# A graph layer on one core: 320 products an edge, selectors that carry all four parts of e, sums turned by VectorE, and a wait of POOL at every other batch

## The chip, the core and the metric

The kernel runs on one core of one Trainium2 chip. The metric is the device time of one execution in microseconds. Three runs of the kernel before took 4756.0, 4765.0 and 4784.8 us; the median is 4765.0 us. Five engines matter: TensorE (PE in the profile; PEld is its weight load), VectorE (DVE), ScalarE (ACT), GpSimd (POOL) and SyncE (SP), which only issues transfers. Matmul results land in PSUM, everything else stands in SBUF.

## The reference

There are 12500 nodes with 160 features and 400000 edges, sorted by destination. A layer norm and a relu come first; the rest, cut to what matters, is:

```python
x0 = h[:, :64];  x1 = h[:, 64:].reshape(n, 32, 3)
y0 = x0 @ W_l1_0 * a / 8
y1 = einsum('nuc,uv->nvc', x1, W_l1_1) * a / sqrt(32)
w = silu(e16 @ fc_W1 / 4) @ fc_W2 / 8            # 192 weights an edge: w_a, w_b (64), w_c, w_d (32)
ys0, ys1 = y0[src], y1[src]                       # the row of the source node
e0, e1 = e4[:, :1], e4[:, 1:]                     # four parts of e
mid_a = w_a * ys0 * e0
mid_d = w_d * einsum('euc,ec->eu', ys1, e1) / sqrt(3)
mid_b = (w_b * ys0)[:, :, None] * e1[:, None, :]
mid_c = (w_c * e0)[:, :, None] * ys1
z0 = zeros((n, 96)).at[dst].add(concat([mid_a, mid_d], 1)) / sqrt(10)
z1 = zeros((n, 96, 3)).at[dst].add(concat([mid_b, mid_c], 1)) / sqrt(10)
out = x + skip(h) + [z0 @ W_l2_0, z1 @ W_l2_1] * a * constants
```

Every edge thus has a weight row (192 numbers), a gathered row of y (160 numbers) and four numbers e. Their products are summed over the edges of a destination.

## The kernel before, in words

The edges lie in 3125 tiles of 128. Four tiles make a batch; there are 782 batches. A first part (the node steps, up to about 115 us) norms the nodes and writes y to memory (`y_d`); in the background the weights are loaded by SP. Then comes the loop over batches, whose order on every engine is written out by hand (a manual schedule): an engine takes its instructions in the order of the program.

In iteration b of that loop stand, in this order:

- `weigh(b + 2)`: PE makes the 192 weights of the batch after next in PSUM (tile `pw`, two buffers; line 606). Then `scale` lets ACT multiply the first 96 weights of each tile by e0 (line 524, four instructions) and copy the other numbers of e and the place in the window into `pw` (line 525).
- for the first three batches of a group the steps `turn`, `linear` and `add` of the group before it: `turn` transposes the sums by PE against an identity (line 656) and ACT copies them (`za`, line 658); `linear` multiplies them by the last weights `wo` (line 665); `add` moves them to their nodes (line 677). `accumulate` lets VectorE add them to `acc` (line 688).
- some work on nodes beside it (the skip path; rows of 16 batches that are computed instead of gathered).
- `select(b + 1)` and `products(b + 1)` on VectorE. `select` makes, for each edge, a 32-wide one-hot row of its place in a window of 32 nodes (line 618) and three copies of it multiplied by e1 (line 620): tile `sel`, 4 x 32 columns. `products` makes 256 products an edge (tile `pr`): lines 530 and 532 for the dot product of ys1 and e1, line 533 for w_b ys0, line 534 for w_a ys0, line 535 for w_c ys1, line 537 for mid_d.
- `sums(b)`: for each tile one matmul of `sel` (stationary, 128 columns) with `pr` (moving, 256 columns) into a window's PSUM tile `pz` (two buffers; line 640). Quadrant 3 of `pz` then holds the sums under the plain one-hot and quadrants 0 to 2 those times e1, of which only parts are used. A window takes 24 tiles at the start of the sorted edges and 3 at their end. When one ends, ACT copies the four useful pieces to `zs` (lines 646 and 648). Four windows are a group.
- `gather(b + 4)`: POOL issues four indirect DMAs (line 573), one a tile, each for 128 rows of y. The first of them waits for the last matmul of `sums(b)` (lines 576 to 579). Each also waits until VectorE has left its buffer of `yg` (six buffers).
- at every fourth batch `hidden_pair`: PE and ACT make the hidden layer for four batches (lines 586 and 591).

fp32 matmuls stand twice in the profile, so 3125 calls at line 640 are 6250 records. A last part of the kernel (from line 892) handles edges outside their window in a loop that runs zero times or once.

Of the kernel before, what the change touches and what calls it, by code (L numbers as in the profile page):

```python
# [10 lines left out]
F32 = mybir.dt.float32  # L11
I32 = mybir.dt.int32
AF = mybir.ActivationFunctionType
# [12 lines left out]
PC = 256  # L26
ZC = 384
# [23 lines left out]
def kernel(  # L51
# [85 lines left out]
    wo = const.tile([P, 3, D], F32, name="wo")  # L137
# [11 lines left out]
    wor = ip.tile([P, 3, D], F32, name="wor")  # L149
# [115 lines left out]
    def edge_weight_loads():  # L265
# [14 lines left out]
        load(wor[0:M0 + M1, 0, 0:M0], w_l2_0)  # L280
        for rows, k, c in ((slice(96, P), 0, 0), (slice(0, 32), 1, 1), (slice(32, 64), 1, 2)):
            load(wor[rows, k, o1(c)], w_l2_1[M0:, :])
        for rows, k, c in ((slice(64, P), 1, 0), (slice(0, 64), 2, 1), (slice(64, P), 2, 2)):
            load(wor[rows, k, o1(c)], w_l2_1[0:M0, :])
# [5 lines left out]
    def edge_weights():  # L290
# [3 lines left out]
        nc.vector.tensor_scalar(wo[M0:M0 + M1, 0, 0:M0], wo[M0:M0 + M1, 0, 0:M0], 1.0 / math.sqrt(3.0), None, ALU.mult)  # L294
# [226 lines left out]
    def scale(pw, ev, n):  # L521

        for k in range(n):
            nc.scalar.activation(pw[:, k, 0:96], pw[:, k, 0:96], AF.Copy, scale=ev[:, k, 0:1])  # L524
        nc.scalar.activation(pw[:, :n, NW:NW + 4], ev[:, :n, 1:5], AF.Copy)  # L525

    def multiply(pr, tmp, wt, yg, n):

        y1 = yg[:, :n, M0:].rearrange("p t (c u) -> p t c u", c=3)
        nc.vector.tensor_tensor(tmp[:, :n, 0:3, :], y1, wt[:, :n, NW:NW + 3].unsqueeze(3).to_broadcast([P, n, 3, M1]),  # L530
                                ALU.mult)
        nc.vector.tensor_reduce(tmp[:, :n, 3, :], tmp[:, :n, 0:3, :].rearrange("p t c u -> p t u c"), AX.X, ALU.add)  # L532
        nc.vector.tensor_mul(pr[:, :n, 192:PC], wt[:, :n, 96:160], yg[:, :n, 0:M0])  # L533
        nc.vector.tensor_mul(pr[:, :n, 0:M0], wt[:, :n, 0:M0], yg[:, :n, 0:M0])  # L534
        nc.vector.tensor_mul(pr[:, :n, 96:192].rearrange("p t (c u) -> p t c u", c=3),  # L535
                             wt[:, :n, M0:96].unsqueeze(2).to_broadcast([P, n, 3, M1]), y1)
        nc.vector.tensor_mul(pr[:, :n, M0:96], wt[:, :n, 160:NW], tmp[:, :n, 3, :])  # L537

    with (
        tc.tile_pool(name="selp", bufs=4) as selp,  # L540
        tc.tile_pool(name="prod", bufs=3) as prod,
        tc.tile_pool(name="tmp", bufs=1) as tmpp,
# [8 lines left out]
        hids, rows, wts, sels, z_ps, z_sb, zT, o_sb, prs, sums_ps, summed = ({} for _ in range(11))  # L551
# [16 lines left out]
        def gather(b):  # L568
# [3 lines left out]
            for k, t in enumerate(tiles_of(b)):  # L572
# [3 lines left out]
                if k == 0 and b - AHEAD in summed:  # L576
# [37 lines left out]
        def select(b):  # L614

            n, wt = slots_of(b), wts[b]
            sel = sels[b] = selp.tile([P, GT, 4, WN], F32, name="sel")[:, :n, :, :]
            nc.vector.tensor_tensor(sel[:, :, 3, :], iota[:, 0:WN].unsqueeze(1).to_broadcast([P, n, WN]),  # L618
                                    wt[:, :n, NW + 3:NW + 4].to_broadcast([P, n, WN]), ALU.is_equal)
            nc.vector.tensor_tensor(sel[:, :, 0:3, :], sel[:, :, 3:4, :].to_broadcast([P, n, 3, WN]),  # L620
                                    wt[:, :n, NW:NW + 3].unsqueeze(3).to_broadcast([P, n, 3, WN]), ALU.mult)

        def products(b):
            wt, yg = wts.pop(b), rows.pop(b)
            pr = prod.tile([P, GT, PC], F32, name="pr")
            tmp = tmpp.tile([P, GT, 4, M1], F32, name="tmp")
            multiply(pr, tmp, wt, yg, slots_of(b))
            prs[b] = pr

        def sums(b):  # L630
# [3 lines left out]
            for k, t in enumerate(tiles_of(b)):  # L634
# [397 lines left out]
```

## Time and profile before

| | |
|---|---|
| median of three runs | 4765.0 us |
| the profiled execution | 4775.0 us, of which the span of its instructions is 4773.1 us |
| batches, tiles, gathers by POOL, windows | 782, 3125, 3061, 598 |
| share of the span that PE, DVE, ACT, POOL are busy | 78%, 62%, 46%, 62% |
| mean busy share of the 16 DMA engines in the loop | about 25% |

The page of the profile gives, in its second part, the share that every engine is busy in 40 equal slices. Nearly all slices look alike:

```profile
PE   7777778787777777777777777778777887788877
DVE  5666666666666666656566656656566666666655
ACT  5333334344444443444444444444444455555555
POOL 5666666666656666666666666656665666665655
```

So no engine is busy throughout, and there is no stage that is much different from the others; ACT has more to do towards the end, where windows are short. A row of the fifth part names a line of the kernel, an engine, the operation, the tiles written and read, shapes and count, then busy time in us and the mean of one in ns, and after the second bar the time that the engine was idle right before such instructions and what ended it ("issue" is an end that the profile doesn't explain by another instruction, "remote" a semaphore whose writer it doesn't know). The timeline lists instructions in order of time with start, length, and in brackets the idle time before them.

### The profile page before, as it was taken

The numbers are of one execution on the slowest core, as the hardware profiler recorded it, in microseconds if no ns is written. First come the engines' busy times: TensorE is split into PE (matmuls) and PEld (weight loads), VectorE is DVE, ScalarE is ACT, GpSimd is POOL, SyncE is SP. The second block draws the span as 40 slices with busy tenths as digits, with TensorE's granted clock in tenths as the row PEclk, the third lists the DMA queues.
The fourth block names the chain that finished last, engine by engine and source line by source line (L and its number), as shares of the span: only waits on it lengthen the run. The fifth ranks groups of instructions, "written<-read, shape, count | busy, mean of one in ns | idle before, by whom it ended". The sixth has DMA issues, their size and how long they took to land.

```text
span 4773.1 us, 53679 instructions
## 1 busy us (share of the span) xinstructions
PE 3720.7 (78%) x13928; PEld 2551.0 (53%) x13928; DVE 2953.5 (62%) x8027; ACT 2205.2 (46%) x7512; POOL 2962.3 (62%) x3145
## 2 busy tenths in 40 slices
PE   7777778787777777777777777778777887788877
PEld 6455555455555554555555555555555555555555
DVE  5666666666666666656566656656566666666655
ACT  5333334344444443444444444444444455555555
POOL 5666666666656666666666666656665666665655
PEclk8888888888988888888888888888888888988988
DMA  7222222222222222222222222222222222222224
GB/s 192 67 60 64 63 62 65 60 65 66 61 62 65 66 70 66 66 63 69 65 69 63 66 62 64 67 62 64 62 66 65 64 66 63 68 66 66 64 58 115
DMA packets 262414, 328.99 MB, mean 69 GB/s; under 512 B 82776, under 2 KB 212104, under 8 KB 262104
## 3 DMA queue, kind: packets, MB, share of 16 engines
q0 software_dynamic: 150128, 256.23, 21.8%
q1 hardware_dynamic: 111478, 69.00, 5.2%
q8 instruction: 113, 1.85, 0.2%
q14 instruction: 197, 1.61, 0.1%
q10 hardware_dynamic: 498, 0.30, 0.0%
HBM read 307.66 MB, written 17.61 MB: 68 GB/s over the span
## 4 chain that ended last, share of the span: by engine, by line
PE 56%; another core or an unknown queue 15%; ACT 12%; issue 8%; DVE 7%; POOL 0%; DMA 0%; DVEq 0%; SPq 0%; ACTq 0%
PE pz L640 23%; PE pw L606 17%; ACT pw L524 6%; PE px L586 6%; PE px L665 3%; ACT zs L648 2%; PE px L656 2%; PE px L677 2%; DVE tmp L532 1%; DVE tmp L530 1%; ACT zs L646 1%; DVE pr L535 1%; DVE pr L534 1%; ACT pw L525 1%
## 5 line engine op out<-in xcount | busy, mean ns | idle before, releaser
L573 POOL DMA_INDIRECT yg<-y_d,src_q x3061 | 2896.2, 946 | 1748.8 <-issue 787.3
L640 PE MATMUL pz<-pr,sel 128*128 128x256 f32 x6250 | 1682.1, 417 | 38.1 <-ACT zs L648 36.1
L606 PE MATMUL pw<-w,hT 128*128 128x384 f32 x3126 | 1314.2, 547 | 304.3 <-DVE pr L537 111.7
L524 ACT ACTIVATE pw<-pw,ev 128x96 f32<-128x96 f32 x3125 | 984.9, 315 | 1199.1 <-remote 303.9
L640 PEld LDWEIGHTS pz<-pr,sel 128*128 128x128 f32 x6250 | 1289.4, 214 | 279.0 <-ACT zs L648 46.4
L606 PEld LDWEIGHTS pw<-w,hT 128*128 128x128 f32 x3126 | 619.2, 208 | 822.5 <-issue 377.2
L618 DVE TENSOR_TENSOR sel<-iota,pw 128x128 f32<-128x128 f32 x782 | 221.5, 283 | 1255.8 <-ACT pw L525 680.1
L646 ACT ACTIVATE zs<-pz 32x192 f32<-32x192 f32 x598 | 193.4, 323 | 801.0 <-remote 345.2
L532 DVE TENSOR_REDUCE tmp<-tmp 128x128 f32<-128x384 f32 x782 | 463.6, 593 | 31.1 <-remote 3.6
L586 PE MATMUL px<-xe,w 32*128 32x512 f32 x782 | 334.2, 750 | 161.0 <-ACT za L658 102.8
L620 DVE TENSOR_TENSOR sel<-sel,pw 128x384 f32<-128x384 f32 x782 | 432.7, 553 | 39.8 <-remote 8.0
L530 DVE TENSOR_TENSOR tmp<-yg,pw 128x384 f32<-128x384 f32 x766 | 419.6, 548 | 55.4 <-DMA yg<-y_d,src_q 48.8
L535 DVE TENSOR_TENSOR pr<-pw,yg 128x384 f32<-128x384 f32 x766 | 419.2, 547 | 0.0
L648 ACT ACTIVATE zs<-pz 32x64 f32<-32x64 f32 x1794 | 383.1, 214 | 24.4
L656 PE MATMUL px<-ident,zs 128*128 128x128 f32 (+1 forms) x450 | 129.3, 362 | 301.3 <-ACT zs L646 259.2
L533 DVE TENSOR_TENSOR pr<-pw,yg 128x256 f32<-128x256 f32 x766 | 317.0, 414 | 0.0
L534 DVE TENSOR_TENSOR pr<-pw,yg 128x256 f32<-128x256 f32 x766 | 316.9, 414 | 0.0
L591 ACT ACTIVATE hT<-px 128x512 f32<-128x512 f32 x391 | 216.1, 594 | 212.2 <-PE px L586 86.7
L656 PEld LDWEIGHTS px<-ident,zs 128*128 128x128 f32 (+1 forms) x450 | 69.7, 159 | 411.9 <-ACT zs L646 307.7
L586 PEld LDWEIGHTS px<-xe,w 32*128 32x128 f32 x782 | 90.2, 218 | 282.3 <-ACT za L658 123.4
L665 PEld LDWEIGHTS px<-wo,za 128*128 128x128 f32 x900 | 163.6, 222 | 108.0 <-ACT hT L591 36.2
L537 DVE TENSOR_TENSOR pr<-pw,tmp 128x128 f32<-128x128 f32 x782 | 219.2, 280 | 0.0
(139 smaller groups left out, 2210.2 us busy)
## 6 DMA issues: line engine op xcount, KB each, us to landing
yg<-y_d,src_q POOLq DMA_INDIRECT x3061
xe<-in_e SPq DMA_DIRECT2D x784, 32.0 KB
xs<-in_x SPq DMA_DIRECT2D x48, 160.0 KB
acc<-in_x SPq DMA_DIRECT2D x11, 640.0 KB
y_d<-ys SPq DMA_DIRECT2D x11, 640.0 KB
out<-acc SPq DMA_DIRECT2D x11, 640.0 KB
raw<-in_e SPq DMA_DIRECT2D x32, 192.0 KB
src_q<-in_src SPq DMA_DIRECT2D x32, 48.0 KB
```

The costliest lines, as they stand in the source:

```text
L524: nc.scalar.activation(pw[:, k, 0:96], pw[:, k, 0:96], AF.Copy, scale=ev[:, k, 0:1])
L530: nc.vector.tensor_tensor(tmp[:, :n, 0:3, :], y1, wt[:, :n, NW:NW + 3].unsqueeze(3).to_broadcast([P, n, 3, M1]), ALU.mult)
L532: nc.vector.tensor_reduce(tmp[:, :n, 3, :], tmp[:, :n, 0:3, :].rearrange("p t c u -> p t u c"), AX.X, ALU.add)
L533: nc.vector.tensor_mul(pr[:, :n, 192:PC], wt[:, :n, 96:160], yg[:, :n, 0:M0])
L534: nc.vector.tensor_mul(pr[:, :n, 0:M0], wt[:, :n, 0:M0], yg[:, :n, 0:M0])
L535: nc.vector.tensor_mul(pr[:, :n, 96:192].rearrange("p t (c u) -> p t c u", c=3), wt[:, :n, M0:96].unsqueeze(2).to_broadcast([P, n, 3, M1]) ...
L573: fetch = nc.gpsimd.indirect_dma_start(out=yg[:, slot(t), :], out_offset=None, in_=y_d, in_offset=bass.IndirectOffsetOnAxis(ap=ev4[t // BL ...
L586: nc.tensor.matmul(ph, w1[r, :], xe[r, :], start=True, stop=True)
L606: nc.tensor.matmul(pw[:, 2 * k:2 * k + m, 0:NW], hT[:, o:o + P], w2[:, :m, :], start=True, stop=True)
L620: nc.vector.tensor_tensor(sel[:, :, 0:3, :], sel[:, :, 3:4, :].to_broadcast([P, n, 3, WN]), wt[:, :n, NW:NW + 3].unsqueeze(3).to_broadcast ...
L640: mm = nc.tensor.matmul(pz[:, 0:PC], sel[:, slot(t), :, :], pr[:, slot(t), :], start=o == 0, stop=last)
L648: nc.scalar.activation(zs[:, 192 + M0 * c:192 + M0 * (c + 1)], pz[WN * c:WN * (c + 1), 192:PC], AF.Copy)
```

## The change

Products are 320 an edge in place of 256, and they are no longer multiplied by any part of e. The products are w_a ys0 (64), w_c ys1 (96), w_b ys0 (64) and w_d ys1 (96). The selector `sel` now has four 32-wide parts: the one-hot row times e0 and times each part of e1. One matmul of 320 columns gives all sums for all four parts; the useful squares are picked when they are turned. The multiplication by e0 on ACT is gone, and so is the dot product on VectorE: both now happen in the sum and in `wo`, which has five slices of 128 rows in place of three.

When a window ends, VectorE transposes its PSUM tile in squares of 32 straight into `za` (two instructions, 128 x 160 and 32 x 160). ACT's copies to `zs`, PE's transposes and ACT's copy of these are gone. `turn` as a step is gone; `linear` and `add` stand at the second and third batch of a group as before, and `linear` has five matmuls.

POOL waits for sums only where b is even. Three more small loads of weights are issued by SP in the node steps.

```diff
-PC = 256
-ZC = 384
+PC = 320
+ZC = 448
+ZK = 5
...
     def scale(pw, ev, n):
-        for k in range(n):
-            nc.scalar.activation(pw[:, k, 0:96], pw[:, k, 0:96], AF.Copy, scale=ev[:, k, 0:1])
-        nc.scalar.activation(pw[:, :n, NW:NW + 4], ev[:, :n, 1:5], AF.Copy)
+        nc.scalar.activation(pw[:, :n, NW:NW + 5], ev[:, :n, :], AF.Copy)
...
     def multiply(pr, wt, yg, n):
         y1 = yg[:, :n, M0:].rearrange("p t (c u) -> p t c u", c=3)
-        nc.vector.tensor_tensor(tmp[:, :n, 0:3, :], y1, wt[:, :n, NW:NW + 3].unsqueeze(3).to_broadcast([P, n, 3, M1]),
-                                ALU.mult)
-        nc.vector.tensor_reduce(tmp[:, :n, 3, :], tmp[:, :n, 0:3, :].rearrange("p t c u -> p t u c"), AX.X, ALU.add)
-        nc.vector.tensor_mul(pr[:, :n, 192:PC], wt[:, :n, 96:160], yg[:, :n, 0:M0])
-        nc.vector.tensor_mul(pr[:, :n, 0:M0], wt[:, :n, 0:M0], yg[:, :n, 0:M0])
-        nc.vector.tensor_mul(pr[:, :n, 96:192].rearrange("p t (c u) -> p t c u", c=3),
-                             wt[:, :n, M0:96].unsqueeze(2).to_broadcast([P, n, 3, M1]), y1)
-        nc.vector.tensor_mul(pr[:, :n, M0:96], wt[:, :n, 160:NW], tmp[:, :n, 3, :])
+        nc.vector.tensor_mul(pr[:, :n, :].rearrange("p t (x u) -> p t x u", x=2)[:, :, :, 0:M0],
+                             wt[:, :n, 0:NW].rearrange("p t (x u) -> p t x u", x=2)[:, :, :, 0:M0],
+                             yg[:, :n, 0:M0].unsqueeze(2).to_broadcast([P, n, 2, M0]))
+        for x in range(2):
+            nc.vector.tensor_mul(pr[:, :n, D * x + M0:D * (x + 1)].rearrange("p t (c u) -> p t c u", c=3),
+                                 wt[:, :n, 96 * x + M0:96 * (x + 1)].unsqueeze(2).to_broadcast([P, n, 3, M1]), y1)
...
-                if k == 0 and b - AHEAD in summed:
+                if k == 0 and b % 2 == 0 and b - AHEAD in summed:
                     tc.add_manual_dep(fetch.ins, summed[b - AHEAD],
...
         def products(b):
+            n, wt, yg = slots_of(b), wts.pop(b), rows.pop(b)
+            own = selp.tile([P, GT, WN], F32, name="own")
+            nc.vector.tensor_tensor(own[:, :n, :], iota[:, 0:WN].unsqueeze(1).to_broadcast([P, n, WN]),
+                                    wt[:, :n, NW + 4:NW + 5].to_broadcast([P, n, WN]), ALU.is_equal)
+            nc.vector.tensor_tensor(sel, own[:, :n, :].unsqueeze(2).to_broadcast([P, n, 4, WN]),
+                                    wt[:, :n, NW:NW + 4].unsqueeze(3).to_broadcast([P, n, 4, WN]), ALU.mult)
+            multiply(pr, wt, yg, n)
...
                 if last:
                     if w == 0:
-                        z_sb[g] = post.tile([P, ZC], F32, name="zs")
-                    pz, zs = z_ps.pop((g, w)), z_sb[g][WN * w:WN * (w + 1), :]
-                    nc.scalar.activation(zs[:, 0:192], pz[96:P, 0:192], AF.Copy)
-                    for c in range(3):
-                        nc.scalar.activation(zs[:, 192 + M0 * c:192 + M0 * (c + 1)],
-                                             pz[WN * c:WN * (c + 1), 192:PC], AF.Copy)
-        def turn(g):
-            m, zs = WN * windows_of(g), z_sb.pop(g)
-            pt = p_x.tile([P, 3, P], F32, name="px")
-            for k in range(3):
-                nc.tensor.transpose(pt[:, k, :m], zs[:m, P * k:P * (k + 1)], ident[:m, :m])
-            za = post.tile([P, 3, P], F32, name="za")
-            nc.scalar.activation(za[:, :, :m], pt[:, :, :m], AF.Copy)
-            zT[g] = za
+                        zT[g] = post.tile([P, ZK, P], F32, name="za")
+                    pz, at_w = z_ps.pop((g, w)), slice(WN * w, WN * (w + 1))
+                    nc.vector.transpose(zT[g][:, :, at_w], pz[:, D:PC].rearrange("p (k u) -> p k u", k=ZK))
+                    nc.vector.transpose(zT[g][0:32, :, at_w], pz[0:32, 0:D].rearrange("p (k u) -> p k u", k=ZK))
...
-            for k in range(3):
-                nc.tensor.matmul(po[:m, :], za[:, k, :m], wo[:, k, :], start=k == 0, stop=k == 2)
+            for k in range(ZK):
+                nc.tensor.matmul(po[:m, :], za[:, k, :m], wo[:, k, :], start=k == 0, stop=k == ZK - 1)
...
-            if g and k < K:
-                (turn, linear, add)[k](g - 1)
+            if g and 0 < k < K:
+                (linear, add)[k - 1](g - 1)
```

The loads of `wo` and the last part of the kernel (edges outside their window) follow the new layout; they are left out here.

More of the change, by code (lines that the diff above doesn't have):

```diff
@@ L148 @@
     wsr = ip.tile([P, 3 * M1], F32, name="wsr")
-    wor = ip.tile([P, 3, D], F32, name="wor")
+    wor = ip.tile([P, ZK, D], F32, name="wor")
     def rows_of_windows():
@@ L278, in o1 @@
             return slice(M0 + M1 * c, M0 + M1 * (c + 1))
[L280 to L284, printed above, removed]
+        load(wor[0:32, 0:2, 0:M0], w_l2_0[0:M0, :].rearrange("(k p) u -> p k u", p=32))
+        for c in range(3):
+            q = slice(32 * (c + 1), 32 * (c + 2))
+            load(wor[0:32, 2 + c, o1(c)], w_l2_1[M0:, :])
+            load(wor[q, 0:2, o1(c)], w_l2_1[0:M0, :].rearrange("(k p) u -> p k u", p=32))
+            load(wor[q, 2 + c, 0:M0], w_l2_0[M0:, :])
         load(ws0[0:M0, :], w_sc0)
@@ L550 @@
     ):
-        hids, rows, wts, sels, z_ps, z_sb, zT, o_sb, prs, sums_ps, summed = ({} for _ in range(11))
+        hids, rows, wts, sels, z_ps, zT, o_sb, prs, sums_ps, summed = ({} for _ in range(10))
         xss, hss, sTs, sps, ohs, ohTs, vals, xTs = ({} for _ in range(8))
```

67 lines of the change are left out of this document (33 added, 34 removed).

## The prediction

> **What bounds the kernel now.** I read the page first: span, busy times, and the engines' shares of the chain of work that ended last.
>
> ```profile
> span 4773.1 us, 53679 instructions
> PE 3720.7 (78%) x13928; PEld 2551.0 (53%) x13928; DVE 2953.5 (62%) x8027; ACT 2205.2 (46%) x7512; POOL 2962.3 (62%) x3145
> PE 56%; another core or an unknown queue 15%; ACT 12%; issue 8%; DVE 7%; POOL 0%; DMA 0%; DVEq 0%; SPq 0%; ACTq 0%
> ```
>
> PE is the fullest engine, yet idle for 4773.1 - 3720.7 = 1052 us, 22%. The chain puts POOL at 0%. Its own row says more, so I took the timeline of POOL next:
>
> ```profile
> L573 POOL DMA_INDIRECT yg<-y_d,src_q x3061 | 2896.2, 946 | 1748.8 <-issue 787.3 <-remote 337.3 <-PE pz L640 254.1
> ```
>
> ```profile
> 1271.42 0.94 POOL L573 DMA_INDIRECT yg<-y_d,src_q  x1 [1.27 <-DVE neg L170]
> ...
> 1275.16 0.94 POOL L573 DMA_INDIRECT yg<-y_d,src_q  x1 [0.30 <-issue]
> 1278.10 0.94 POOL L573 DMA_INDIRECT yg<-y_d,src_q  x1 [1.99 <-PE pw L606]
> ...
> 1286.84 0.94 POOL L573 DMA_INDIRECT yg<-y_d,src_q  x1 [0.30 <-issue]
> 1289.89 0.94 POOL L573 DMA_INDIRECT yg<-y_d,src_q  x1 [2.11 <-remote]
> ...
> 1303.64 0.95 POOL L573 DMA_INDIRECT yg<-y_d,src_q  x1 [0.30 <-issue]
> 1307.29 0.94 POOL L573 DMA_INDIRECT yg<-y_d,src_q  x1 [2.71 <-PE pw L606]
> ```
>
> A gather takes 0.946 us and the next follows 0.30 us later: 5.0 us a batch, and 4645 us of the span is POOL gathering or idle between gathers. It goes in runs that end at a wait for sums: here one of 4 gathers, one of 8, one of 12, with pauses of 1.99, 2.11 and 2.71 us behind them. Counted so over the span there are 110 runs of 4 (mean pause 2.38 us), 185 of 8 (2.11), 88 of 12 (2.84), 7 of 16 (4.82) and 6 others: 396 pauses. Per gather that is 1.77, 1.48, 1.46 and 1.53 us; all together (2896.2 + 1748.8)/3061 = 1.517 us.
>
> Then the timeline of PE and ACT about the last of these pauses:
>
> ```profile
> 1298.49 1.36 ACT L524 ACTIVATE pw<-pw,ev 128x96 f32<-128x96 f32 x4 [2.01 <-PE pw L606]
> ...
> 1299.30 1.53 PE L606 MATMUL pw<-w,hT 128*128 128x384 f32 x4
> ...
> 1304.32 1.53 PE L606 MATMUL pw<-w,hT 128*128 128x384 f32 x4 [1.76 <-DVE pr L537]
> 1307.11 1.36 ACT L524 ACTIVATE pw<-pw,ev 128x96 f32<-128x96 f32 x4 [7.04 <-PE pw L606]
> ...
> 1309.09 1.03 PE L656 MATMUL px<-ident,zs 128*128 128x128 f32 x3 [3.25 <-ACT zs L646]
> ```
>
> The weights that PE finished at 1299.30 + 1.53 = 1300.83 are taken up by ACT at 1307.11, 6.3 us later, with ACT idle. PE's word of completion seems to be held up while POOL runs on, and to come through when POOL has paused: POOL's last gather ended at 1304.59, ACT goes at 1307.11, POOL at 1307.29. This is my reading of timings; the rows name no cause. So neither engine is the bound alone: POOL pauses for sums, and after a pause PE still has to wait for ACT and VectorE to make products from weights that were ready long before.
>
> **The change part by part.**
>
> VectorE first.
>
> ```profile
> L532 DVE TENSOR_REDUCE tmp<-tmp 128x128 f32<-128x384 f32 x781 | 463.4, 593 | 31.1 <-remote 3.6 <-DVE tmp L530 0.8
> L620 DVE TENSOR_TENSOR sel<-sel,pw 128x384 f32<-128x384 f32 x781 | 432.4, 554 | 39.8 <-remote 8.0 <-DVE sel L618 3.2 <-issue 2.1
> L530 DVE TENSOR_TENSOR tmp<-yg,pw 128x384 f32<-128x384 f32 x765 | 419.4, 548 | 55.4 <-DMA yg<-y_d,src_q 48.8 <-issue 6.4
> L535 DVE TENSOR_TENSOR pr<-pw,yg 128x384 f32<-128x384 f32 x765 | 418.9, 548 | 0.0
> L533 DVE TENSOR_TENSOR pr<-pw,yg 128x256 f32<-128x256 f32 x765 | 316.8, 414 | 0.0
> L618 DVE TENSOR_TENSOR sel<-iota,pw 128x128 f32<-128x128 f32 x781 | 221.3, 283 | 1255.8 <-ACT pw L525 680.1 <-ACT pw L524 415.9 <-issue 69.0
> L537 DVE TENSOR_TENSOR pr<-pw,tmp 128x128 f32<-128x128 f32 x781 | 219.1, 280 | 0.0
> L688 DVE SCALAR_TENSOR_TENSOR acc<-px,a_sb,acc 128x160 f32 x300 | 114.6, 382 | 149.4 <-PE px L677 71.8 <-PE pz L640 28.0 <-remote 21.5
> L421 DVE TENSOR_SCALAR h<-acc,mv 128x160 f32<-128x160 f32 x98 | 26.4, 311 | 11.9 <-remote 6.7 <-PE po L455 2.6 <-DVE mv L418 0.6
> L736 DVE TENSOR_TENSOR oh<-iota,xp 128x512 f32<-128x512 f32 x16 | 11.0, 689 | 0.0
> ```
>
> A batch costs 0.283 (line 618) + 0.554 + 0.548 + 0.593 + 2 x 0.414 (533, and 534 of the same shape) + 0.548 + 0.280 = 3.63 us. After, it is 0.283, two of 512 elements (selector; products with ys0) at 0.689, two of 384 at 0.548: 2.76 us. The saving is 782 x 0.87 = 684 us. The transposes come on top, 2 x 598 windows. No row is a transpose of VectorE. The nearest have 160 elements too: 0.311 us out of SBUF, 0.382 us with PSUM; above, the rearranged read of line 532 at 0.593. As many elements a partition pass in any of these, so nothing speaks for less than 0.311. I take 0.382 for its PSUM: 457 us (372 to 709). VectorE's total falls to about 2953 - 684 + 457 = 2726 us; it stays off the bound.
>
> ACT loses nearly all of this:
>
> ```profile
> L524 ACT ACTIVATE pw<-pw,ev 128x96 f32<-128x96 f32 x3125 | 984.9, 315 | 1199.1 <-remote 303.9 <-PE pw L606 303.5 <-issue 219.0
> L525 ACT ACTIVATE pw<-ev 128x16 f32<-128x16 f32 x781 | 146.4, 187 | 24.7
> L646 ACT ACTIVATE zs<-pz 32x192 f32<-32x192 f32 x598 | 193.4, 323 | 801.0 <-remote 345.2 <-PE pz L640 257.1 <-issue 72.1
> ```
>
> Line 525 stays with 20 elements for 16, at the same cost. The path from ready weights to ready products, 4 x 0.315 + 0.187 + 3.63 = 5.08 us now, becomes 0.187 + 2.76 = 2.94 us, 2.1 us or 42% shorter. That is what counts, since it is what PE waits for after a pause.
>
> PE gets more work:
>
> ```profile
> L640 PE MATMUL pz<-pr,sel 128*128 128x256 f32 x6250 | 1682.1, 417 | 38.1 <-ACT zs L648 36.1 <-issue 2.0
> L606 PE MATMUL pw<-w,hT 128*128 128x384 f32 x3124 | 1313.7, 548 | 304.3 <-DVE pr L537 111.7 <-issue 69.4 <-DVE pr L535 56.6
> L586 PE MATMUL px<-xe,w 32*128 32x512 f32 x782 | 334.2, 750 | 161.0 <-ACT za L658 102.8 <-issue 25.4 <-remote 17.4
> L665 PE MATMUL px<-wo,za 128*128 128x160 f32 x894 | 171.5, 335 | 46.3 <-ACT hT L591 28.3 <-ACT za L658 14.9 <-DVE acc L731 1.7
> L656 PE MATMUL px<-ident,zs 128*128 128x128 f32 x447 | 128.7, 363 | 301.2 <-ACT zs L646 259.2 <-issue 23.9 <-ACT hT L591 6.6
> ```
>
> The sums grow by 64/256 of 1682.1: +420 us. Five `linear` matmuls for three: +114. The transposes go: -129. PE's busy time becomes 4127 us at the same clock. Of its 1052 us idle I take away 301 (line 656, which waits for `zs` right after the sums; `linear`, next in line, stands a batch later, behind one more batch of weights and sums, now (1313.7 + 1682.1)/782 = 3.8 us), 103 (line 586 behind `za`), and of the 112 + 57 before line 606 that VectorE's products end the 42%, 71 us. Left: 577 us. The sum by PE is 4704 us at the old clock.
>
> The clock is not fixed:
>
> ```profile
> core 0: 4773.1 us, clock 0.868
> 3600.00:3800.00 200.00, 164.20 (x583) 109.23 (x579) 122.03 (x332) 98.78 (x343) 122.86 (x131) 0.83 0.26 65
> 4000.00:4200.00 200.00, 164.74 (x636) 112.96 (x634) 130.28 (x353) 111.78 (x398) 127.59 (x136) 0.91 0.26 65
> ```
>
> Two stretches of 200 us with PE equally busy (the first sum in each row) were granted 0.83 and 0.91. These bound it: 4316 + 577 = 4893 us and 3937 + 577 = 4514 us. With idle time cut by 45% I take 0.89, nearer the upper row: 4025 + 577 = 4602 us. The Trainium skill, "TensorE: Matmul & The Clock Gate", Part 1, says that the clock is either half or full, and that a window of about 3.4 us without work halves it. Were no idle stretch so long, PE's sum by that rule would be 4127 x 0.868 + 577 = 4159 us, and POOL's would bind; the mean of 0.868 fits a mix of the two, but no row here shows what would end it.
>
> POOL waits at even batches only, so runs of 4 and 12 can no longer come (but beside the 16 batches that are not gathered). All in eights at 1.477 us: 3061 x 1.477 + 128 (the span outside the 4645) = 4649 us. On odd batches POOL still waits for a `yg` buffer, left by products of six batches before: long done.
>
> SP issues three more small weight loads in the node steps, and POOL clears a wider `wor`, beside PE's and ACT's work on the nodes, which sets the pace there: nothing. Uncovered it is three issues of 5.01/7 = 0.7 us:
>
> ```profile
> 999.54 5.01 SPq L363 DMA_DIRECT2D xe<-in_e  x7
> ```
>
> Between 4602 (PE) and 4649 (POOL), nearer the latter, I put the span at 4640 us. The profiled execution took 2 us more than its span and was 10 us over the median: 4632 us as a median, 2.8% less.
>
> **The rivals.**
>
> *VectorE stands at the transposes (slower).* VectorE takes instructions in order, and `products(b + 2)` is queued behind the transposes of `sums(b)`. These wait for a word from PE of the kind that came 6.3 us late; before, ACT bore that wait and only `scale(b + 3)` stood behind it. PE waits for these products. Price: 396 pauses x 5.08 us would be 2012 us, and PE is idle 1052, so 52% of such a path is paid now. With the transposes in it the path is 2.94 + 2 x 0.382 = 3.70 us; 52% of it at 383 pauses is 737 us, in place of 577, and without a better clock the span is 4864 us. It decides once PE's idle time passes 4813 - 4127 = 686 us. For it speaks that windows are short late (598 in 782 batches); against it, that many batches of the early half end no window. The Trainium skill, "PSUM — Partial Sum Buffer", Engine vs sequencer instructions, calls VectorE's queue strictly first in, first out; the trace shows no instruction out of order.
>
> *Longer holds (no change).* If words from PE come only at pauses, sparser pauses hold them longer. Runs of 16 with their 4.82 us cost 1.533 us a gather, 4821 us in all; half and half with eights 1.505 us, 4735 us. Here, too, belongs that the dropped wait is not the one that acts.
>
> *POOL sets the pace (much faster).* If PE keeps up over 16 gathers and half of them go so with 2.11 us behind (1.364 us each), the mean is 1.42 us: 4475 us.
>
> **How the numbers follow.** About 1% (4717 to 4813 us) is what a measurement can tell from no change. My forecast gets 0.48, with a range of its own from 4500 to 4717 us; the much faster case 0.08; no change 0.22; VectorE at the transposes 0.22. Faster is 0.56, same 0.22, slower 0.22. The range goes from 4450 us, under the much faster case, to 4860 us, about the price of the slower one.
>
> **What would show it.** Line 640's successor should take about 2100 us at the old clock, the new transposes near 0.38 us each, idle time of PE near 580 us, the clock near 0.89, and POOL's timeline runs of 8 and 16 with pauses near 2 us. I am wrong if VectorE's idle time before the transposes is large and PE's idle time before the weights grows, if pauses behind eights are 3 us or more, or if PE's clock falls.

## The result, and the profile after

The changed kernel took 5045.8 us (median of 4 runs, 5020.1 to 5059.7) against 4770.4 us for the kernel before in the same session: 1.057 times as long, with a 95% interval of 1.051 to 1.063. The forecast was 4632 us, and its range ended at 4860 us.

The page of the changed kernel, its span, busy times and the shares of the chain of waits:

```profile
span 5057.8 us, 46909 instructions
...
PE 3868.3 (76%) x14078; PEld 2519.7 (50%) x14078; DVE 2725.4 (54%) x6877; ACT 584.7 (12%) x1845; POOL 2963.6 (59%) x3145
...
PE 51%; another core or an unknown queue 23%; DVE 11%; issue 11%; ACT 2%; ACTq 1%; POOL 1%; DVEq 0%; DMA 0%; SPq 0%; POOLq 0%
```

The work on ACT and VectorE fell as meant (ACT 2205 to 585 us, VectorE 2954 to 2725), PE is 148 us busier, and every engine is idle for longer. PE's idle time is 5057.8 - 3868.3 = 1190 us, 137 us more than before. The rest of the story is in the groups of instructions, from the view that keeps shapes apart:

```profile
L570 POOL DMA_INDIRECT yg<-y_d,src_q x3061 | 2897.5, 947 | 2035.2 <-PE pz L633 858.5 <-issue 832.7 <-remote 152.7
L633 PE MATMUL pz<-pr,sel 128*128 128x320 f32 x6250 | 1998.3, 466 | 50.6 <-DVE za L640 46.5 <-DVE za L639 3.3 <-issue 0.5
L603 PE MATMUL pw<-w,hT 128*128 128x384 f32 x3124 | 1255.0, 527 | 440.2 <-DVE pr L534 363.8 <-issue 37.9 <-DVE ev L775 25.2
L534 DVE TENSOR_TENSOR pr<-pw,yg 128x384 f32<-128x384 f32 x1530 | 773.1, 546 | 0.0
...
L619 DVE TENSOR_TENSOR sel<-own,pw 128x512 f32<-128x512 f32 x781 | 536.6, 687 | 27.0
L530 DVE TENSOR_TENSOR pr<-pw,yg 128x512 f32<-128x512 f32 x765 | 522.5, 683 | 40.9 <-DMA yg<-y_d,src_q 32.0 <-issue 8.8
...
L639 DVE STREAM_TRANSPOSE za<-pz 128x160 f32<-128x160 f32 x598 | 206.5, 345 | 1558.9 <-remote 894.7 <-PE pz L633 382.3 <-issue 124.4
L640 DVE STREAM_TRANSPOSE za<-pz 32x160 f32<-32x160 f32 x598 | 202.1, 338 | 20.5
L617 DVE TENSOR_TENSOR own<-iota,pw 128x128 f32<-128x128 f32 x781 | 199.2, 255 | 158.2 <-ACT pw L525 86.7 <-issue 52.3 <-ACT hT L588 14.0
L658 PE MATMUL px<-os,place 128*128 128x160 f32 x596 | 159.3, 405 | 548.8 <-ACT os L648 444.4 <-issue 94.4 <-ACT hT L588 10.0
L525 ACT ACTIVATE pw<-ev 128x20 f32<-128x20 f32 x781 | 149.2, 191 | 2706.7 <-PE pw L603 1103.4 <-issue 545.8 <-remote 543.6
```

Three readings. POOL's idle time ahead of its gathers grew from 1748.8 to 2035.2 us, as much as the span did (286 of 285 us). The part of it that waits for the sums themselves grew by more than that, from 254.1 us (line 640) to 858.5 us (line 633), while the part put down to "remote" fell from 337.3 to 152.7 us. VectorE now stands 1558.9 us ahead of the first transpose, and PE has a new stand of 548.8 us at `add` (line 658), whose predecessor, line 677, had 55.1.

Counted over the timeline of POOL as in the prediction, there are 21 runs of 4 gathers, 98 of 8 (mean pause 2.66 us), 5 of 12, 134 of 16 (mean pause 6.30 us) and 8 others. Seven gathers of ten now stand in runs of 16, which were 7 runs before, and the pause behind these is 6.30 us where the seven had 4.82. One such pause, on the timeline of all engines:

```profile
3716.41 1.92 PEld L633 LDWEIGHTS pz<-pr,sel 128*128 128x128 f32 x8
3716.50 2.35 PE L633 MATMUL pz<-pr,sel 128*128 128x320 f32 x8
...
3718.68 1.45 PE L603 MATMUL pw<-w,hT 128*128 128x384 f32 x4
...
3723.45 0.95 POOL L570 DMA_INDIRECT yg<-y_d,src_q  x1 [0.30 <-issue]
3725.87 0.30 ACT L648 ACTIVATE os<-px 128x160 f32<-128x160 f32 x1 [9.60 <-remote]
...
3726.23 1.43 PE L658 MATMUL px<-os,place 128*128 128x160 f32 x4 [6.10 <-issue]
...
3727.45 4.47 PE L633 MATMUL pz<-pr,sel 128*128 128x320 f32 x8
...
3732.20 0.94 POOL L570 DMA_INDIRECT yg<-y_d,src_q  x1 [7.80 <-PE pz L633]
```

POOL issues the last of 16 gathers at 3723.45. ACT's copy `os` reads what `linear` had finished about ten microseconds earlier, and it starts at 3725.87, 1.5 us after the last gather ended. Then PE, which has stood for 6.10 us at `add`, goes on, and only after another 4.47 us of sums does POOL get what it waits for. So the 7.80 us are made of two parts: 1.5 us until the words come (a word is the step of a semaphore by which one engine tells the others that it is done), and 6.3 us of work that PE has yet to do. In that part the eight records of sums take 4.47 us; eight such records took 2.35 us eleven microseconds before. The busy times and the granted clock in three windows (the columns are the window, its length, busy time of PE, PEld, DVE, ACT and POOL, the granted clock, the DMA share and GB/s):

```profile
3716.40:3718.90 2.50, 2.50 (x12) 1.84 (x11) 0.00 (x0) 0.00 (x0) 1.89 (x3) 1.00 0.26 69
3718.90:3726.20 7.30, 1.23 (x4) 0.38 (x2) 0.00 (x0) 0.30 (x1) 4.28 (x5) 0.92 0.24 64
3726.20:3731.90 5.70, 5.67 (x13) 4.10 (x14) 4.33 (x11) 0.19 (x1) 0.00 (x0) 0.50 0.00 0
```

After 6.1 us without a matmul PE works at half its clock for 5.7 us, with POOL waiting on it. The Trainium skill, "TensorE: Matmul & The Clock Gate", Part 1, says that an idle window of about 3.4 us halves the clock; these rows agree that an idle window halves it (1.00, then 0.50, after 6.1 us), but don't show how short a window would do. Stretches of over 5 us without a matmul, counted after the node steps, were 57 before (368 us) and are 123 now (944 us).

### The profile page after: what moved, and what is told of

It reads as the page before. It is cut to its first block, busy times and chain, and to the rows that moved or that the text cites. A ratio compares the mean times of both kernels' runs of the same rounds, so it can differ in the third digit from the quotient of the medians.

```text
span 5057.8 us, 46909 instructions
## 1 busy us (share of the span) xinstructions
PE 3868.3 (76%) x14078; PEld 2519.7 (50%) x14078; DVE 2725.4 (54%) x6877; ACT 584.7 (12%) x1845; POOL 2963.6 (59%) x3145
## 4 chain that ended last, share of the span: by engine, by line
PE 51%; another core or an unknown queue 23%; DVE 11%; issue 11%; ACT 2%; ACTq 1%; POOL 1%; DVEq 0%; DMA 0%; SPq 0%; POOLq 0%
PE pz L633 24%; PE pw L603 15%; DVE pr L534 4%; PE px L583 3%; PE px L658 3%; PE px L646 3%; DVE pr L530 2%; ACTq L525 1%; DVE za L639 1%; DVE za L640 1%; DVE own L617 1%; POOL yg L570 1%; PE po L457 1%; ACT hT L588 1%
## 5 line engine op out<-in xcount | busy, mean ns | idle before, releaser
L570 POOL DMA_INDIRECT yg<-y_d,src_q x3061 | 2897.5, 947 | 2035.2 <-PE pz L633 858.5
L633 PE MATMUL pz<-pr,sel 128*128 128x320 f32 x6250 | 1998.3, 466 | 50.6 <-DVE za L640 46.5
L603 PE MATMUL pw<-w,hT 128*128 128x384 f32 x3126 | 1255.5, 527 | 440.2 <-DVE pr L534 363.8
L639 DVE STREAM_TRANSPOSE za<-pz 128x160 f32<-128x160 f32 x598 | 206.5, 345 | 1558.9 <-remote 894.7
L534 DVE TENSOR_TENSOR pr<-pw,yg 128x384 f32<-128x384 f32 x1532 | 773.5, 546 | 0.0
L658 PE MATMUL px<-os,place 128*128 128x160 f32 x600 | 160.1, 405 | 549.2 <-ACT os L648 444.8
L619 DVE TENSOR_TENSOR sel<-own,pw 128x512 f32<-128x512 f32 x782 | 536.9, 687 | 27.0
L530 DVE TENSOR_TENSOR pr<-pw,yg 128x512 f32<-128x512 f32 x766 | 522.8, 682 | 40.9 <-DMA yg<-y_d,src_q 32.0
L525 ACT ACTIVATE pw<-ev 128x20 f32<-128x20 f32 x782 | 149.3, 191 | 2708.9 <-PE pw L603 1105.6
L617 DVE TENSOR_TENSOR own<-iota,pw 128x128 f32<-128x128 f32 x782 | 199.4, 255 | 158.2 <-ACT pw L525 86.7
L646 PE MATMUL px<-wo,za 128*128 128x160 f32 x1500 | 245.4, 314 | 11.2 <-ACT hT L588 10.7
L583 PE MATMUL px<-xe,w 32*128 32x512 f32 x782 | 229.2, 647 | 5.9 <-remote 5.9
L640 DVE STREAM_TRANSPOSE za<-pz 32x160 f32<-32x160 f32 x598 | 202.1, 338 | 20.5
```

The costliest lines, as they stand in the source:

```text
L530: nc.vector.tensor_mul(pr[:, :n, :].rearrange("p t (x u) -> p t x u", x=2)[:, :, :, 0:M0], wt[:, :n, 0:NW].rearrange("p t (x u) -> p t x u ...
L534: nc.vector.tensor_mul(pr[:, :n, D * x + M0:D * (x + 1)].rearrange("p t (c u) -> p t c u", c=3), wt[:, :n, 96 * x + M0:96 * (x + 1)].unsqu ...
L570: fetch = nc.gpsimd.indirect_dma_start(out=yg[:, slot(t), :], out_offset=None, in_=y_d, in_offset=bass.IndirectOffsetOnAxis(ap=ev4[t // BL ...
L583: nc.tensor.matmul(ph, w1[r, :], xe[r, :], start=True, stop=True)
L603: nc.tensor.matmul(pw[:, 2 * k:2 * k + m, 0:NW], hT[:, o:o + P], w2[:, :m, :], start=True, stop=True)
L619: nc.vector.tensor_tensor(sel, own[:, :n, :].unsqueeze(2).to_broadcast([P, n, 4, WN]), wt[:, :n, NW:NW + 4].unsqueeze(3).to_broadcast([P, ...
```

## The experiments

The theory was that the sparser wait is to blame: POOL runs on for 16 gathers, PE's words of completion come late, and the backlog is paid in one long pause. The rivals were that VectorE standing at the transposes costs the time, or that the new work (320 products, five matmuls in `linear`) does. Each session ran the kernel before beside the others, on another chip each time.

**First session of experiments.** The first kernel is the changed one with POOL's wait put back at every batch:

```diff
-                if k == 0 and b % 2 == 0 and b - AHEAD in summed:
+                if k == 0 and b - AHEAD in summed:
```

> The changed kernel with POOL's wait for sums put back at every batch; all else of the change stays. Theory H (PE's word of completion is held up while POOL gathers back to back, and the sparser wait lengthens POOL's runs and so the holds): runs of 16 vanish, the pauses behind runs fall from a mean of 4.5 us to about 2.3 us, PE's idle time before line 658 falls from 549 us to under 150 us, and the time is 4550 to 4750 us, under the kernel before. Rival V (the time comes from the new work itself, VectorE standing at the transposes and 25% more columns on PE): the time stays at 4950 to 5050 us.

Measured: 3956.1 us; ratio to the kernel before 0.9993 (0.9984 to 1.0003). The kernel before itself took 3959.4 us here, 17% less than in the session of the result. Neither theory had allowed for that.

The second is the kernel before with the wait at every other batch, the same condition the other way round:

```diff
-                if k == 0 and b - AHEAD in summed:
+                if k == 0 and b % 2 == 0 and b - AHEAD in summed:
```

> The kernel before with one edit: POOL waits for sums at even batches only. Theory H: runs of 4 and 12 go over into 8 and 16, holds get longer, PE's idle time grows where it waits for ACT (transposes of zs, line 656), and the time rises by 3 to 8%, to 4900 to 5150 us. Rival V: POOL waits less and nothing else changes, so the time is the same or up to 3% lower, 4630 to 4790 us.

Measured: 3958.9 us, 1.0003 (0.9994 to 1.0013).

The third is the changed kernel with a wait at every gather, for its own tile's sums:

```diff
-                if k == 0 and b % 2 == 0 and b - AHEAD in summed:
-                    tc.add_manual_dep(fetch.ins, summed[b - AHEAD],
+                if (b - AHEAD, k) in summed:
+                    tc.add_manual_dep(fetch.ins, summed[b - AHEAD, k],
...
-                summed[b] = mm.ins.name
+                summed[b, k] = mm.ins.name
```

> The changed kernel with a wait at every gather: each waits for the matmul of its own tile four batches before. Theory H: POOL is stopped for a moment many times, runs are short, words of PE get through, and the time is 4300 to 4650 us, if short pauses are enough to let them through; with runs of 1 to 3 gathers the mean hold at a word is under 0.5 us. Rival V: 4950 to 5050 us as the changed kernel, or more, since POOL waits more often.

Measured: 3955.4 us, 0.999 (0.998 to 0.9999).

The fourth is the changed kernel without POOL's gathers. SP loads as many rows of y in their order, so the gathering of the source rows is left out:

```diff
-            for k, t in enumerate(tiles_of(b)):
-                fetch = nc.gpsimd.indirect_dma_start(
-                    out=yg[:, slot(t), :], out_offset=None, in_=y_d,
-                    in_offset=bass.IndirectOffsetOnAxis(ap=ev4[t // BLK][6][:, t % BLK:t % BLK + 1], axis=0))
-                if k == 0 and b % 2 == 0 and b - AHEAD in summed:
+            n = len(tiles_of(b))
+            r0 = b * GT * P % (N - GT * P) // P * P
+            fetch = nc.sync.dma_start(yg[:, 0:n, :], by_tile(y_d[r0:r0 + n * P, :]))
+            if b % 2 == 0 and b - AHEAD in summed:
...
```

> The changed kernel with the gathers left out: for each batch SP fetches 512 rows of y in order (not the source rows) by one plain transfer, with the same wait at even batches. POOL issues nothing in the loop. Theory H in its narrow form (POOL's gathers are what holds PE's words): the holds vanish, PE's idle time falls under 400 us and the time is 4050 to 4400 us. If the words are held by something of PE's own, or by the traffic of rows, PE's idle time stays near 1190 us and the time over 4800 us.

Measured: 3520.1 us, 0.889 (0.887 to 0.891).

Why do the three with gathers agree within 0.1%? Groups of the first of them, `every_batch`:

```profile
L570 POOL DMA_INDIRECT yg<-y_d,src_q x3061 | 2901.4, 948 | 944.3 <-issue 681.6 <-PE pw L603 110.0 <-DVE za L640 23.8
...
L530 DVE TENSOR_TENSOR pr<-pw,yg 128x512 f32<-128x512 f32 x765 | 528.0, 690 | 941.7 <-DMA yg<-y_d,src_q 940.9
```

POOL gathers in runs of 444, 2548 and 69 with one short pause between each, and VectorE waits 940.9 us for the rows. A gather every (2901.4 + 944.3)/3061 = 1.256 us, 3846 us in all, sets the time of whatever kernel it feeds. In every trace of this kind PE's words come at once: 0.014 us after the end of a matmul in the median. ACT, where it stands idle for PE's weights, starts on them 0.09 us after PE's last matmul.

In the session of the result that was so only while POOL paused or was early in a run. In the trace of the changed kernel, and where ACT stood idle, it started 0.14 us after PE's end in the mean where that end fell in the first four gathers of a run, 0.90 us in the fifth to eighth (the median is still 0.09), and 5.83 us in the ninth to twelfth (67 cases). The other engines' words were not late there: VectorE, idle for ACT's copy, started 0.03 us after it at whatever gather (55 cases), and PE, idle for VectorE's products, 0.05 to 0.33 us after them (108 cases). So it is PE's words that come late, and not every engine's. Since the ends of matmuls are modelled in the profile, it can't tell a late word from a matmul that ends later than shown. I call these late words holds, and a session with them one with holds.

**Second session.** Is it the changed kernel as a whole that is different here, or the session? The changed kernel ran as it is, and the kernel before with the same plain rows (the edit as above, with its own wait at every batch).

> The changed kernel as it is, measured beside the kernel before once more. In the first experiments the kernel before took 3959 us in place of 4770, and PE's words were not held up. Theory H: the 5.7% come from the holds and nothing else. Where words are not held, POOL's gathers bind both kernels (3061 x 1.25 us and what lies around them) and the ratio is 0.995 to 1.005 at 3950 to 3965 us; where they are held, it is 1.04 to 1.07 at about 5040 us. Rival V (the new work itself costs time): the ratio is over 1.03 in either case.

Measured: 3952.6 us, 0.9985 (0.9976 to 0.9995). The kernel before took 3958.8 us. So the session, not the kernel, made the difference: without holds the change is worth nothing.

> The kernel before with the gathers left out: for each batch SP fetches 512 rows of y in order (not the source rows) by one plain transfer that waits for the sums of four batches before. With the changed kernel treated so at 3520 us, PE busy 99%, this prices the change without POOL. If PE then binds here too, the time is 3250 to 3350 us (PE's work less the 25% more columns and two linear matmuls, plus the transposes), and the change costs PE 5 to 8%. If the longer path over ACT and VectorE binds in place of PE, the time is 3400 us or more and the change is worth something once POOL is out of the way.

Measured: 3276.9 us, 0.828 (0.826 to 0.829). Lines of its page and its groups, then of the changed kernel with plain rows:

```profile
PE 3156.1 (96%) x13928; PEld 2297.1 (70%) x13928; DVE 2918.4 (89%) x8027; ACT 2202.8 (67%) x7512; POOL 66.0 (2%) x84
...
L639 PE MATMUL pz<-pr,sel 128*128 128x256 f32 x6250 | 1488.1, 381 | 0.0
```

```profile
PE 3466.6 (99%) x14078; PEld 2311.5 (66%) x14078; DVE 2715.0 (77%) x6877; ACT 591.6 (17%) x1845; POOL 66.1 (2%) x84
...
L632 PE MATMUL pz<-pr,sel 128*128 128x320 f32 x6250 | 1818.4, 434 | 0.6 <-DVE za L639 0.6
```

With no gathers to wait for, PE is the bound in both, and the change makes PE's work 310 us longer: 3520.1/3276.9 = 1.074 (two sessions, whose kernels before took 3959.4 and 3958.8 us). Most of it is the sums, 1818.4 for 1488.1 us. The change moves work onto the engine that is next in line. While POOL's gathers bind at 3957 us, that is hidden.

**Third session.** What makes a hold? One theory was that steps of semaphores crowd each other on their way while POOL issues gathers (P), the other that holds belong to the chip or session (Q). P can be tried: the kernel before with five, and with ten, small loads more in each batch, each with its steps of a semaphore (their data are not used).

```diff
...
+            fl = flp.tile([P, 5], F32, name="fl")
+            for i in range(5):
+                nc.sync.dma_start(fl[:, i:i + 1], x[0:P, i:i + 1])
```

> The kernel before with five small transfers more for each batch on SP (128 rows of 4 bytes from x into a scratch tile that nobody reads): 80 more semaphore steps a batch. The trace of the profiled run before holds 23519 semaphore updates, that of the same program with no holds some 80000, so the holds and the lost records go together. Theory P (the path that carries and records semaphore updates is overfull when words are held): with 80 more steps in some 5 us the holds come back, the time is over 4200 us and the trace loses updates. Theory Q (the holds belong to the chip or the session of the first measurement): the time stays at 3940 to 3990 us.

Measured: 3959.9 us, 1.0005 (0.9994 to 1.0016).

> The same with ten small transfers for each batch, five on SP and five on ACT: 160 more semaphore steps a batch. Theory P: holds, as in the run with five, over 4300 us. Theory Q: under 4000 us, since ACT has room for five issues a batch.

Measured: 4006.5 us, 1.012 (1.009 to 1.015), and PE's words came after 0.014 us in the median in both traces. The traces record 140,689 and 195,660 steps of semaphores, against some 75,000 to 81,000 without the loads. P finds no support: ten loads cost 1.2%, but brought no holds on this chip.

The two kernels with the wait changed ran here again in hope of a session with holds, which it wasn't.

> The changed kernel with POOL's wait at every batch, once more, for the case that this chip holds PE's words. With holds, theory H: 4550 to 4750 us, runs of 16 gone; rival V: 4950 to 5050 us. Without holds both say 3950 to 3960 us.

> The kernel before with POOL's wait at even batches only, once more, for the case that this chip holds PE's words. With holds, theory H: 4900 to 5150 us; rival V: 4630 to 4790 us. Without holds both say 3950 to 3965 us.

Measured: 3957.0 us, 1.0003 (0.9992 to 1.0014), and 3955.8 us, 0.9994 (0.9983 to 1.0005).

**Fourth session.** The same three kernels once more, on a fourth chip.

> The changed kernel as it is, a gauge for the session. If the holds belong to the session or the chip, this draw either has them or hasn't: with them the kernel before takes about 4770 us and this one about 5050 us (ratio near 1.057, POOL in runs of 16 with pauses above 6 us); without them both take about 3955 us (ratio 0.998 to 1.000, POOL in runs of hundreds). If the holds came from something else that passes with time, such as the way the first runs were recorded, no draw will show them again.

Measured: 5015.5 us, 1.048 (1.044 to 1.052); the kernel before took 4781.0 us. The holds were back, and with them the result.

> The changed kernel with the wait at every batch again. In a session with holds: if the sparser wait is to blame, 4630 to 4770 us, no slower than the kernel before; if the transposes on VectorE and the longer sums are to blame, 4950 to 5050 us. In a session without holds: 3957 us, as twice before, and it tells nothing.

Measured: 4701.8 us, 0.984 (0.981 to 0.987).

> The kernel before with the wait at every other batch. In a session with holds: if the sparser wait is to blame, 4950 to 5050 us; if not, 4740 to 4820 us. In a session without holds: 3957 us, and it tells nothing.

Measured: 5000.1 us, 1.046 (1.042 to 1.049).

Both times lie in the range that was set for the case that the sparser wait is to blame, and this settles which part of the change it is. The sparser wait alone costs 4.6%; all the rest of the change, with the wait left as it was, gains 1.6%, and is the fastest of the four kernels. On top of that rest the sparser wait costs more, 5015.5/4701.8 = 1.067. Lines of the changed kernel with the wait at every batch (span, busy times, and groups):

```profile
span 4707.3 us, 46910 instructions
...
PE 3876.4 (82%) x14078; PEld 2527.1 (54%) x14078; DVE 2736.5 (58%) x6877; ACT 582.4 (12%) x1845; POOL 2961.6 (63%) x3145
```

```profile
L570 POOL DMA_INDIRECT yg<-y_d,src_q x3061 | 2895.6, 946 | 1685.7 <-issue 793.6 <-PE pz L633 389.9 <-remote 311.7
...
L603 PE MATMUL pw<-w,hT 128*128 128x384 f32 x3124 | 1237.7, 521 | 223.5 <-DVE pr L534 142.0 <-issue 34.8 <-ACT hT L588 29.8
...
L639 DVE STREAM_TRANSPOSE za<-pz 128x160 f32<-128x160 f32 x598 | 206.3, 345 | 1321.9 <-PE pz L633 564.5 <-remote 439.8 <-PE pw L603 124.0
...
L658 PE MATMUL px<-os,place 128*128 128x160 f32 x596 | 121.8, 332 | 93.0 <-ACT os L648 80.4 <-issue 12.6
```

And groups of the kernel before with the wait at every other batch:

```profile
L573 POOL DMA_INDIRECT yg<-y_d,src_q x3061 | 2905.6, 949 | 1969.8 <-issue 806.7 <-PE pz L640 758.3 <-remote 145.9
...
L606 PE MATMUL pw<-w,hT 128*128 128x384 f32 x3124 | 1298.0, 542 | 453.5 <-DVE pr L537 249.2 <-remote 52.2 <-issue 45.6
...
L677 PE MATMUL px<-os,place 128*128 128x160 f32 x596 | 135.1, 357 | 268.5 <-ACT os L667 252.2 <-ACT hT L591 11.6 <-issue 4.8
```

Read POOL's row first: its wait for the sums is 758.3 us with the sparser wait and no other part of the change, 389.9 us with everything but that, 858.5 with both and 254.1 with neither (the last two from the session of the result; with both it was 880.6 us in this one). PE's stand at `add` goes the same way: 268.5, 93.0, 548.8 and 55.1. So does PE's stand ahead of the weights: 453.5, 223.5, 440.2 and 304.3. VectorE's stand ahead of the transposes does not: it is 1321.9 us in the fastest kernel.

POOL's timeline was counted in these four traces (the first and last row are from the session of the result, the others from this one): the pauses, and for each the time from the end of the last gather to PE's first recorded word on one of its semaphores, then the time from there to POOL's next gather.

| kernel, session with holds | runs of 4, 8, 12, 16 | pause behind 16 (us) | to the first word, then | mean clock |
|---|---|---|---|---|
| before | 110, 185, 88, 7 | 4.82 | 1.82, 3.00 | 0.868 |
| before, every other batch | 19, 162, 6, 101 | 6.65 | 2.41, 4.24 | 0.865 |
| changed, every batch | 112, 67, 132, 32 | 3.70 | 2.27, 1.43 | 0.911 |
| changed | 21, 98, 5, 134 | 6.30 | 2.42, 3.88 | 0.880 |

By these counts the runs of 12 are what the sparser wait turns into runs of 16. Behind the 132 runs of 12 in the third row the pause is 2.53 us, 2.05 to the first word and 0.49 then. The first word comes about 2 us after POOL stops behind runs of 12 and of 16 alike; about a fifth of PE's words have no record in these traces, so it can come earlier than shown. What grows is the part behind it, from 0.5 us to about 4: the work that PE couldn't do for want of words, done while POOL waits. In the 134 long pauses of the changed kernel PE is busy for 3.66 of the 6.30 us, at a mean granted clock of 0.62.

Gaps of over 5 us without a matmul, counted as above, were 32 (219 us) with the wait at every batch and 123 (944 us) with the change as it is.

**Fifth session.** Three kernels were to show the dose and the mechanism: the wait at every fourth batch (`b % 4 == 0`), POOL setting a spare tile to zero before the gathers of a batch, and the wait at every gather again. It was a session without holds.

```diff
...
             rows[b] = yg
+            nc.gpsimd.memset(idle, 0.0)
             for k, t in enumerate(tiles_of(b)):
...
-                if k == 0 and b % 2 == 0 and b - AHEAD in summed:
+                if k == 0 and b - AHEAD in summed:
```

> The changed kernel with the wait at every fourth batch. In a session with holds (before near 4780 us): if the length of POOL's runs sets the hold, runs of 16 and 32 with pauses of 6 us and more: 5100 to 5500 us, the slowest of all; if runs end by themselves at about 16 gathers, as before_other_batch_3 and changed_3 would also allow, about 5020 us as the changed kernel. In a session without holds: 3955 us like every other version.

Measured: 3963.7 us, 0.9991 (0.9981 to 1.0001).

> The changed kernel with the wait at every batch, and POOL sets a spare tile of 128x1024 to zero before the gathers of each batch (about 1.1 us by the 517 ns of 128x480). The output is unchanged. In a session with holds: if words come through whenever POOL issues no transfer, each batch gives them 1.4 us, the pauses shrink to little and the time is 4100 to 4600 us, less than every_batch_3's 4702; if POOL has to stand idle, the 782 x 1.1 us come on top: up to 5560 us. In a session without holds, POOL's gathers set the pace and it is 3957 + 860 = about 4820 us.

Measured: 4594.8 us, 1.158 (1.156 to 1.160). Groups of it:

```profile
L572 POOL DMA_INDIRECT yg<-y_d,src_q x3061 | 2903.1, 948 | 832.0 <-issue 806.7 <-PE pz L635 5.6 <-DMA drel_d<-drel 5.2
...
L570 POOL MEMSET idle<- 128x1024 f32 x766 | 742.8, 970 | 0.2
```

The 742.8 us of POOL's new work come back as 4594.8 - 3967.3 = 628 us (860 was expected, at 1.1 us each for the 0.970 measured); nearly all of the rest is idle time between gathers, 944.3 us in `every_batch` and 832.0 us here. Where POOL issues without pause, what it does is the time of the kernel.

> The changed kernel with a wait at every gather, for its own tile's matmul of four batches before. In a session with holds: if POOL's pauses are what lets words through and shorter runs are better, 4550 to 4700 us, at or under every_batch_3; if shorter runs only add pauses (1.77 us a gather in runs of 4), 4800 to 5400 us. In a session without holds: 3955 us, as before.

Measured: 3963.0 us, 0.9986 (0.9976 to 0.9995).

## Why the prediction was wrong, point by point

**The step that failed** is the one on POOL: "POOL waits at even batches only, so runs of 4 and 12 can no longer come" and "All in eights at 1.477 us: 3061 x 1.477 + 128". The first held (21 runs of 4 and 5 of 12 are left, of 110 and 88). The second didn't: where runs of 12 had been, runs of 16 stand, not of 8. A gather then cost (16 x 0.947 + 15 x 0.30 + 6.30)/16 = 1.62 us in the runs of 16, and (2897.5 + 2035.2)/3061 = 1.611 us in the mean, where the sum had 1.477.

**"Longer holds" was the right rival, mis-sized.** It named the mechanism (sparser pauses) and took 4.82 us for the pause behind a run of 16. That number was from 7 runs of a kernel that could stop at any batch. With the wait skipped there were 134, and the pause was 6.30 us. Perhaps the 7 were runs in which PE was well ahead; that isn't shown. With 1.62 and 0.70 of the gathers in runs of 16, the rest in eights at (8 x 0.947 + 7 x 0.30 + 2.66)/8 = 1.54, the sum is 3061 x 1.596 + 128 = 5013 us. The rival would have been the slower case, not the unchanged one. That backlog at the pause is the reason for the 16s' longer pause is read from the timeline and the table; no run changed the backlog alone.

**"VectorE stands at the transposes"** had a time nearer the result (4864 us) and was wrong as a cause. VectorE does stand there, 1558.9 us. But with the wait at every batch it stands there 1321.9 us, in a kernel 1.6% faster than the one before. Two of the prediction's own signs pointed to this rival: VectorE's stand is large, and PE's stand ahead of the weights grew from 304.3 to 440.2 us. The second is the sparser wait's too: it is 223.5 us with the transposes and the wait at every batch, and 453.5 us in the kernel before with the sparser wait, where VectorE turns nothing.

**VectorE's sum** came out right partly by luck: 2726 us predicted, 2725.4 measured. The transposes took 206.5 + 202.1 = 408.6 us for 457, at 0.345 and 0.338 us where 0.382 was taken, so all the rest took 48 us more than the sum had, and the two misses cancel. Single rows came out near their terms: the products 0.683 and 0.546 us and the selectors 0.687, for 0.689, 0.548 and 0.689. The path from weights to products came out at 0.191 + 0.255 + 0.687 + 0.683 + 2 x 0.546 = 2.91 us (2.94 predicted).

**PE's busy time** was set too high, PE's idle time too low. The busy time is 3868 us at 0.880, where 4127 us at 0.868 was the sum. The sums took 1998.3 us where 2102 were in the sum, 19% more than the 1682.1 of the kernel before and not 25%; with plain rows, at a clock above 0.99 in both kernels, it was 22%. The hidden layer's matmuls fell from 334.2 to 229.2 us, which the sum didn't have. The idle time is 1190 us for 577. The 71 us taken off ahead of the weights didn't go: 304.3 us became 440.2. Line 656's 301 us did go, but `add` came in its place with 548.8: its left operand is ACT's copy of `linear`, which I had said stands a batch later without asking who waits for it in turn. With the wait at every batch this is 93.0 us and PE's idle time 4707.3 - 3876.4 = 831 us, so 359 of the 613 us by which it was set too low go with the sparser wait. Of the clock I forecast 0.89; it was 0.880, and 0.911 with the wait at every batch, where long gaps are fewest.

**SP's loads and POOL's clearing of a wider `wor`** left nothing to see, as said.

With its wait at every batch the kernel runs in 4702 us in a session with holds. So the forecast's sign was right for the rest of the change, which brings 1.6% there; the 2.8% of the forecast was too much, and PE's idle time is still 831 us there for the 577 taken.

**What stays open.** What makes a session one with holds isn't known. The session of the result and one of five later ones had them, the chips differ, and more steps of semaphores didn't bring them. Every run left the profiler's records, and the traces with holds lack most of those of semaphores, so that the recording has a part in it isn't ruled out. That PE's words wait for POOL's pauses is a correlation of times in four kernels' traces; the trial with other work on POOL fell into a session without holds, and so did the wait at every fourth batch and at every gather, so the dose beyond every second batch wasn't seen.

## What to carry to other kernels

A wait that looks like pure delay can be what keeps two engines in step (here in sessions with holds): before thinning one out, ask what the engine will do with the freedom, and price the case in which it runs on to the next wait, with the backlog that the others then have, not with the pause seen at such lengths before. Run the kernel before beside every trial and change one thing at a time, since the same pair of kernels differed by 5.7% in one session and by nothing in another; a version that is best or level in both (here the change with the wait at every batch) is the one to keep. Where an engine's issue rate sets the time (1.256 us a gather here), work saved elsewhere is worth nothing until that rate falls, and work moved onto the next bound shows only then (7.4%).

## What the runs showed of the hardware that was not expected

- The same kernel took 4770 to 4781 us in two sessions and 3957 to 3967 us in four. In the slower ones PE's words came late while POOL issued indirect transfers without pause; VectorE's and ACT's didn't in the changed kernel. There ACT started on PE's weights after 0.14 us in the mean at the first four gathers of a run, and after 5.83 us at the ninth to twelfth. In the others it was 0.09 us in the mean. The traces with late words record 20,100 to 23,600 steps of semaphores, the others some 75,000 to 81,000 for kernels of the same kind; most of what is missing are steps by transfers.
- PE at half its clock after 6.1 us without a matmul was seen directly: eight records of sums in 4.47 us against 2.35.
- A transpose of 128 x 160 fp32 out of PSUM in squares of 32 took 345 ns on VectorE, and one of 32 x 160 took 338: a quarter of the partitions saved 7 ns.
- 6250 records of fp32 matmuls took 1488.1 us with 256 columns and 1818.4 us with 320, in kernels without gathers at a granted clock above 0.99. That is 22% more for 25% more columns; the means of single records, whose modelled ends overlap, are 381 and 434 ns (14%).
